# The last step of a spiking recurrence: its final gather as a piece of its own, the reset operand by thirds, Newton's step in two operations

## The chip, the cores and the metric

The kernel runs on one core of a Trainium2 chip. The metric is the device time of one execution in microseconds (us). The time before is the median of three executions. The profile is of one more execution, with a time of its own.

## The reference, cut to what matters

1024 users (B) each have a sequence of 50 item numbers (T). An item number selects a row of a table of 100001 items by 128 features (D); row 0 counts as zeros.

```
e      = emb[seq]                                  # [B, T, D]
uF     = cumsum(e, axis=1) / min(t, length)        # running mean
y      = (uF - mean_B(uF)) * rsqrt(var_B(uF) + 1e-5) * gamma + beta
for t in range(50):                                # v starts at zero
    v = v + (y[:, t] - v) / 2
    spike = (v >= 1);  v = v - spike;  count += spike
scores = (count / 50) @ emb.T                      # [1024, 100001], float32
```

The mean and the variance are taken over the 1024 users, for each feature and each step. The recurrence is short in bytes; the scores are 409.6 MB of output.

## The kernel before, in words

**Layout.** In the recurrence the 128 partitions are the features and the 1024 columns are the users, in eight blocks of 128. PSUM holds the running sums in `pre[0]` and `pre[1]` (512 columns each), the spike counts in `sums[0]` and `sums[1]`, and two buffers of 1024 columns, `v0` and `v1`, in which the steps' `v` alternate: even steps in `v0`, odd ones in `v1`.

**One step t.** GpSimd (POOL) issues eight indirect DMAs for step t+1, one for each block of users (`gather`, L198), into `e`. TensorE (PE) transposes each block of `e` and adds it into `pre` (L307). VectorE (DVE) turns each half of `pre` into the running mean `uF` (L316) and takes its statistics (`bn_stats`, L317), and `bn_aggr` (L327) joins the two halves to mean and variance, `mv`. ScalarE (ACT) takes the square root of the variance (L331) and subtracts the mean from `uF` (L332). DVE forms the scale `a` by four operations of one column after a reciprocal and a Newton step (L340 to L346): `r = 1/r`, `q = r*r`, `q = (var+eps)*q`, `q = 1.5-0.5*q`, `a = q*r*...`. ACT writes the scaled input into `v` (L350, `x`). DVE adds half of the old `v` after its reset (L353, `step`), which needs `negv = spike - v` of the step before (L359).

**The spikes of the step before** are taken by DVE (`s`, L337), and PE adds them into `sums` by a product with the identity (`counted`, L275). In the steps up to 48 this stands between `bn_aggr` and the reciprocal.

**The last step** (t = 49) differs. Its `s` (L301) and its whole `negv` (L302) come first on DVE, ahead of `uF`. `counted` stands on PE behind all eight transposes, and ACT copies `sums` to `count` (L325). Sixteen transposes into a spare tile, `warm` (L376), fill PE's time until the first product. Then the 1024 columns are handled in three groups of 128, 512 and 384: `x` of all three on ACT, then on DVE `step` and `spiked` of the first group (giving `countA`), `step` of the two others, and `spiked` of the two others (`countB`, `countC`, L286). The operands `v` of the groups lie in `pre[0]`, `pre[1]` and `vC`, which takes the buffer `v1`; `warm` takes `v0`.

**The scores.** For every piece of 1024 items the table's rows are transposed (L128) and split into a high and a low part (L150, L151); PE multiplies them with the counts (L158) for eight blocks of users; DVE (L467) and ACT (L469) evict by turns, and SyncE's queue stores (L167). Users of block 0 come first, from `countA`, by four evictions of 512 columns (L401, L403) that use `sums` and a tile `po1` in `v0`. The blocks after it use `countB` and `countC`. Ahead of the recurrence's end two pieces of items have been split already.

**Order.** Each engine runs its instructions in the order in which the program gives them; nothing is rescheduled. A tile's reuse waits for the last instruction that used it.

Of the kernel before, what the change touches and what calls it, by code (L numbers as in the profile page):

```python
# [12 lines left out]
F32 = mybir.dt.float32  # L13
# [5 lines left out]
ALU = mybir.AluOpType  # L19

P = 128
BN_EPS = 1e-5
V_TH = 1.0
HALF = 1024
KQ = HALF // P
BANK = 512
# [10 lines left out]
def rec_kernel(  # L37
# [9 lines left out]
    nc = tc.nc  # L47
    B, T = seq.shape
    N, D = table.shape
    NB = B // P  # L50
# [119 lines left out]
    with ExitStack() as ph:  # L170
        once = ph.enter_context(tc.tile_pool(name="once", bufs=1))
        lp = ph.enter_context(tc.tile_pool(name="lif", bufs=2))
        sp = ph.enter_context(tc.tile_pool(name="stats", bufs=3))
# [3 lines left out]
        vp = ph.enter_context(tc.tile_pool(name="v", bufs=1, space=bass.MemoryType.PSUM))  # L177
# [16 lines left out]

        def gather(t):
            es[t] = gp.tile([P, B], F32, tag="e", name=f"e_{t}")
            for n in range(NB):
                nc.gpsimd.indirect_dma_start(  # L198
                    out=es[t][:, n * P : (n + 1) * P],
                    out_offset=None,  # L200
                    in_=table,
                    in_offset=bass.IndirectOffsetOnAxis(ap=idx[:, n, t : t + 1].bitcast(U32), axis=0),
                )
# [34 lines left out]
        rlen = once.tile([P, B], F32, tag="rlen", name="rlen")  # L238
# [10 lines left out]
        negv = once.tile([P, B], F32, tag="negv", name="negv")  # L249
# [3 lines left out]
        pre = [accp.tile([P, BANK], F32, tag=f"pre{h}", name=f"pre{h}") for h in range(B // BANK)]  # L253
# [19 lines left out]
        def counted(t, s):  # L273
            for h in range(B // BANK):
                nc.tensor.matmul(  # L275
                    sums[h],
                    lhsT=ident_h,
                    rhs=s[:, h * BANK : (h + 1) * BANK],
                    start=t == 0,
                    stop=t == T - 2,  # L280
                    skip_group_check=True,
                )


        def spiked(out, cs, v):
            nc.vector.scalar_tensor_tensor(out, v, V_TH, count[:, cs], ALU.is_ge, ALU.add)  # L286

        whole = slice(0, B)
        halves = [slice(h * BANK, (h + 1) * BANK) for h in range(B // BANK)]
        v = None  # L290
# [3 lines left out]
        for t in range(T):  # L294
            last = t == T - 1
            if t + 1 < T:
                gather(t + 1)
            e = es.pop(t)
            if last:
                s = lp.tile([P, B], BF16, tag="s", name=f"s_{t - 1}")  # L300
                nc.vector.tensor_single_scalar(s, v, V_TH, ALU.is_ge)  # L301
                nc.vector.tensor_tensor(negv, s, v, ALU.subtract)  # L302
            uF = up.tile([P, B], F32, tag="uF", name=f"uF_{t}")
            bs = sp.tile([P, B // BANK, 6], F32, tag="bs", name=f"bs_{t}")
            for h, cs in enumerate(halves):
                for k in range(0, BANK, P):
                    nc.tensor.matmul(  # L307
                        pre[h][:, k : k + P],
                        lhsT=e[:, h * BANK + k : h * BANK + k + P],
                        rhs=ident,  # L310
                        start=False,
                        stop=last,
                        is_transpose=True,
                        skip_group_check=True,
                    )
                nc.vector.scalar_tensor_tensor(uF[:, cs], rlen[:, cs], 1.0 / (t + 1), pre[h], ALU.max, ALU.mult)  # L316
                nc.vector.bn_stats(bs[:, h, :], uF[:, cs])  # L317
            if not last:
                correct(t + 1, l)
            else:  # L320

                counted(t - 1, s)
                count = once.tile([P, B], F32, tag="zT", name="count")
                for h, cs in enumerate(halves):
                    nc.scalar.copy(count[:, cs], sums[h])  # L325
            mv = sp.tile([P, 2], F32, tag="mv", name=f"mv_{t}")
            nc.vector.bn_aggr(mv, bs.rearrange("p h s -> p (h s)"))  # L327


            r = sp.tile([P, 1], F32, tag="r", name=f"r_{t}")  # L330
            nc.scalar.activation(r, mv[:, 1:2], AF.Sqrt, bias=eps)  # L331
            nc.scalar.activation(uF, uF, AF.Identity, bias=mv[:, 0:1], scale=-1.0)  # L332


            if t and not last:
                s = lp.tile([P, B], BF16, tag="s", name=f"s_{t - 1}")
                nc.vector.tensor_single_scalar(s, v, V_TH, ALU.is_ge)  # L337
                counted(t - 1, s)

            nc.vector.reciprocal(r, r)  # L340
            q = sp.tile([P, 1], F32, tag="q", name=f"q_{t}")
            nc.vector.tensor_mul(q, r, r)
            nc.vector.scalar_tensor_tensor(q, mv[:, 1:2], BN_EPS, q, ALU.add, ALU.mult)
            nc.vector.tensor_scalar(q, q, -0.5, 1.5, ALU.mult, ALU.add)
            a = sp.tile([P, 1], F32, tag="a", name=f"a_{t}")
            nc.vector.tensor_scalar(a, q, r, hgb[:, 0:1], ALU.mult, ALU.mult)  # L346


            def x(vt, cs):
                nc.scalar.activation(vt, uF[:, cs], AF.Identity, bias=hgb[:, 1:2], scale=a)  # L350

            def step(vt, cs):
                nc.vector.scalar_tensor_tensor(vt, negv[:, cs], -0.5, vt, ALU.mult, ALU.add)  # L353

            if not last:
                vt = vp.tile([P, B], F32, tag=f"v{t % 2}", name=f"v_{t}")
                x(vt, whole)
                if t:
                    nc.vector.tensor_tensor(negv, s, v, ALU.subtract)  # L359
# [11 lines left out]

        warm = vp.tile([P, HALF], F32, tag="v0", name="warm")
        for k in range(2 * KQ):
            nc.tensor.transpose(warm[:, k % KQ * P : (k % KQ + 1) * P], ident, ident)  # L376
        vC = vp.tile([P, B - BANK - P], F32, tag="v1", name="vC")
        groups = [
            (slice(0, P), pre[0][:, :P], countA),
            (slice(P, P + BANK), pre[1], countB),  # L380
            (slice(P + BANK, B), vC, countC),
        ]
        for cs, vt, _ in groups:
            x(vt, cs)
        cs, vt, first = groups[0]
        step(vt, cs)
        spiked(first, cs, vt)
        for cs, vt, _ in groups[1:]:
            step(vt, cs)
        for cs, vt, c in groups[1:]:  # L390
# [118 lines left out]
```

## Time and profile before

| | |
|---|---|
| median of three runs | 1647.41 us (1646.87 to 1650.15) |
| profiled execution, its own time | 1574.98 us |
| its span, first to last instruction | 1573.2 us |
| mean granted TensorE clock | 0.966 |
| busy shares of the span | PE 73%, DVE 60%, ACT 40%, POOL 24% |
| gathers on POOL | 400 of 945 ns each |
| stores | 409.60 MB written |

The span has two stages. In the first, up to about 505 us, POOL issues one gather after the other and the other engines follow it, at about 10 us a step. In the second the scores are written: between 600 and 700 us the DMA engines are fully busy and move 420 GB/s. The last step of the recurrence and the first products are the joint between the two.

### The profile page before, as it was taken

To read this page: it belongs to the slowest core of one execution; us is meant where nothing else is said; L and a number is where in the kernel's file an instruction comes from. 1 tells how busy PE (TensorE), PEld (TensorE's weight loads), DVE (VectorE), ACT (ScalarE), POOL (GpSimd) and SP (SyncE) were. 2 spreads that over 40 slices of the span, in tenths; PEclk is the share of its full clock that TensorE was granted. 3 is DMA by queue.
4 is the path that set the end of the run, shared out by engine and by line. 5 is a ranking of instruction groups with operands and counts; after the bars stand their busy time and mean duration, and the time that the engine had idled before them with its cause. 6 is when DMAs were issued, how large, how long until landed. Compare 5 with 4: busy or idle time off the path is not lost.

```text
span 1573.2 us, 12601 instructions
## 1 busy us (share of the span) xinstructions
PE 1147.9 (73%) x4538; PEld 817.6 (52%) x4548; DVE 942.1 (60%) x1161; ACT 630.6 (40%) x700; POOL 378.5 (24%) x406
## 2 busy tenths in 40 slices
PE   4555555555555998889878878887888778777885
PEld 2222222222233776668667666666666667665763
DVE  4777777777777665667555545545555555554553
ACT  2322222222233554555444444444444444443442
POOL 6777777777776000000000000000000000000000
PEclk9999999999999999999999999999999999999998
DMA  9622222222221999999999999999999999999898
GB/s 338 247 53 53 53 53 52 53 53 53 53 79 45 385 416 403 423 417 402 426 429 428 430 427 424 421 415 428 418 428 423 414 428 410 426 424 426 362 423 371
DMA packets 54859, 488.14 MB, mean 310 GB/s; under 512 B 12139, under 2 KB 12940, under 8 KB 32524
## 3 DMA queue, kind: packets, MB, share of 16 engines
q1 hardware_dynamic: 33424, 429.81, 65.1%
q0 software_dynamic: 12800, 26.24, 6.3%
q10 hardware_dynamic: 8572, 31.28, 5.0%
q8 instruction: 36, 0.59, 0.1%
q14 instruction: 27, 0.22, 0.0%
HBM read 77.69 MB, written 409.60 MB: 310 GB/s over the span
## 4 chain that ended last, share of the span: by engine, by line
DMA 50%; POOL 19%; PE 11%; issue 10%; ACT 5%; DVE 4%; another core or an unknown queue 0%; DVEq 0%; ACTq 0%; SPq 0%; POOLq 0%
DMA scores<-o 46%; POOL e L198 19%; PE po L158 10%; ACT o L469 4%; DMA e<-in_L_rec_emb_table,idx 3%; DVE o L467 2%; DMA rows<-in_L_rec_emb_table 2%; PE pt L128 1%; PE pre L307 0%; ACT pairs L150 0%; DVE s L337 0%; DVE bs L317 0%; DVE uF L316 0%; DVE pairs L151 0%; DMA idx<-in_r_seq 0%
## 5 line engine op out<-in xcount | busy, mean ns | idle before, releaser
L467 DVE TENSOR_SCALAR o<-po 128x1024 f32<-128x1024 f32 x391 | 464.1, 1220 | 354.3 <-DMA scores<-o 314.5
L469 ACT ACTIVATE o<-po 128x1024 f32<-128x1024 f32 (+1 forms) x391 | 388.1, 1019 | 548.9 <-DMA scores<-o 336.2
L198 POOL DMA_INDIRECT e<-in_L_rec_emb_table,idx x400 | 377.8, 945 | 124.5 <-issue 116.4
L158 PE MATMUL po<-pairs,countB 128*128 128x512 f32 x1136 | 304.6, 415 | 69.0 <-ACT o L469 52.1
L158 PEld LDWEIGHTS po<-pairs,countB 128*128 128x128 f32 x1136 | 218.5, 197 | 132.0 <-ACT o L469 66.8
L307 PE MATMUL pre<-ident,e 128*128 128x128 f32 x400 | 156.2, 452 | 152.4 <-DMA e<-in_L_rec_emb_table,idx 149.0
L158 PE MATMUL po<-pairs,countC 128*128 128x512 f32 x852 | 230.4, 416 | 49.3 <-ACT o L469 49.3
L158 PEld LDWEIGHTS po<-pairs,countC 128*128 128x128 f32 x852 | 163.6, 198 | 94.2 <-ACT o L469 60.5
L307 PEld LDWEIGHTS pre<-ident,e 128*128 128x128 f32 x400 | 79.2, 200 | 246.1 <-DMA e<-in_L_rec_emb_table,idx 223.6
L151 DVE TENSOR_TENSOR pairs<-pt,pairs 128x1024 fp32r<-128x1024 f32 x71 | 86.3, 1222 | 91.3 <-ACT pairs L150 91.2
L331 ACT ACTIVATE r<-mv,eps 128x1 f32<-128x1 f32 x50 | 14.7, 295 | 305.5 <-DVE mv L327 305.5
L316 DVE SCALAR_TENSOR_TENSOR uF<-rlen,pre 128x512 f32<-128x512 f32 x100 | 68.4, 684 | 108.3 <-PE pre L307 108.2
L128 PE MATMUL pt<-ident,rows 128*128 128x128 f32 x782 | 111.7, 290 | 9.7 <-ACT o L469 5.1
L128 PEld LDWEIGHTS pt<-ident,rows 128*128 128x128 f32 x782 | 100.3, 152 | 29.9 <-issue 8.8
L158 PE MATMUL po<-hi,countB 128*128 128x512 f32 x216 | 89.5, 414 | 15.8 <-ACT o L469 12.6
L264 PE MATMUL pre<-zT,l 128*128 128x512 f32 x100 | 78.1, 783 | 18.9 <-DVE uF L316 18.8
L275 PE MATMUL sums<-s,ident_h 128*128 128x512 bf16 x88 | 45.4, 607 | 60.6 <-DVE s L337 60.6
L158 PE MATMUL po<-lo,countB 128*128 128x512 f32 x216 | 86.5, 402 | 0.0
L158 PE MATMUL po<-pairs,countA 128*128 128x512 f32 x284 | 71.7, 395 | 9.3 <-ACT o L469 9.2
L150 ACT CAST pairs<-pt 128x1024 fp32r<-128x1024 f32 x71 | 71.8, 1012 | 15.0 <-PE pt L128 14.8
L158 PE MATMUL po<-hi,countC 128*128 128x512 f32 (+1 forms) x162 | 67.8, 418 | 11.7 <-ACT o L469 11.7
L350 ACT ACTIVATE v<-uF,hgb,a 128x1024 f32<-128x1024 f32 x49 | 59.2, 1208 | 37.6 <-DVE a L346 37.5
(76 smaller groups left out, 841.9 us busy)
## 6 DMA issues: line engine op xcount, KB each, us to landing
scores<-o SPq DMA_DIRECT2D x88, 3072.0 KB, 20.3
scores<-o SPq DMA_DIRECT2D x32, 1536.0 KB, 8.9
scores<-o SPq DMA_DIRECT2D x16, 2048.0 KB, 12.6
scores<-o SPq DMA_DIRECT2D x30, 1024.0 KB, 8.6
rows<-in_L_rec_emb_table ACTq DMA_DIRECT2D x19, 1536.0 KB, 29.3
rows<-in_L_rec_emb_table SPq DMA_DIRECT2D x6, 3072.0 KB, 25.3
scores<-o SPq DMA_DIRECT2D x8, 1872.5 KB, 11.3
e<-in_L_rec_emb_table,idx POOLq DMA_INDIRECT x400, 2.5
```

Source lines behind the costliest of these rows:

```text
L128: nc.tensor.transpose(pt[:, k0 : k0 + kw], r[:kw, k0 : k0 + D], ident[:kw, :kw])
L150: nc.scalar.copy(vh, vp)
L151: nc.vector.tensor_tensor(vl, vp, vh.bitcast(F32), ALU.subtract)
L158: nc.tensor.matmul(po[:, :kw], lhsT=counts[n], rhs=part[:, k0 : k0 + kw], start=j == 0, stop=j == 1,)
L198: nc.gpsimd.indirect_dma_start(out=es[t][:, n * P : (n + 1) * P], out_offset=None, in_=table, in_offset=bass.IndirectOffsetOnAxis(ap=idx[: ...
L264: nc.tensor.matmul(pre[h], lhsT=l, rhs=zT[:, h * BANK : (h + 1) * BANK], start=t == 0, stop=False, skip_group_check=True,)
L275: nc.tensor.matmul(sums[h], lhsT=ident_h, rhs=s[:, h * BANK : (h + 1) * BANK], start=t == 0, stop=t == T - 2, skip_group_check=True,)
L307: nc.tensor.matmul(pre[h][:, k : k + P], lhsT=e[:, h * BANK + k : h * BANK + k + P], rhs=ident, start=False, stop=last, is_transpose=True, ...
L316: nc.vector.scalar_tensor_tensor(uF[:, cs], rlen[:, cs], 1.0 / (t + 1), pre[h], ALU.max, ALU.mult)
L350: nc.scalar.activation(vt, uF[:, cs], AF.Identity, bias=hgb[:, 1:2], scale=a)
L467: nc.vector.tensor_scalar_mul(o[:, h0 : h0 + hw], po[:, :hw], 1.0 / T)
L469: nc.scalar.mul(o[:, h0 : h0 + hw], po[:, :hw], 1.0 / T)
```

## The change

Five things are edited.

- The last gather's order of blocks becomes 0, 1, 2, 3, 5, 6, 7, 4. Its `uF` and `bn_stats` are taken in three pieces: 512 columns (blocks 0 to 3), 384 columns (blocks 5 to 7) and 128 columns (block 4, the one that comes last).
- `counted` of the step before, on PE, moves ahead of the transpose of block 4.
- `negv` of the last step is no longer taken whole ahead of `uF`: the first 128 columns follow `bn_aggr`, the next 512 follow `a`, the last 384 follow `countA`.
- In every step, `ve = var + eps` is formed on DVE right after `bn_aggr`, and the Newton step's two products become one operation, `q = (r*ve)*r`.
- `warm` takes the buffer `v1` in place of `v0`, since the old `v` in `v0` is now read later.

```diff
 def gather(t):
-            for n in range(NB):
+            order = list(range(NB))
+            if t == T - 1:
+                order.append(order.pop(NB // 2))
+            for n in order:
...
+        thirds = [slice(0, P), slice(P, P + BANK), slice(P + BANK, B)]
+
+        def negated(cs):
+            nc.vector.tensor_tensor(negv[:, cs], s[:, cs], v[:, cs], ALU.subtract)
...
                 nc.vector.tensor_single_scalar(s, v, V_TH, ALU.is_ge)
-                nc.vector.tensor_tensor(negv, s, v, ALU.subtract)
...
-            for h, cs in enumerate(halves):
-                for k in range(0, BANK, P):
+            pieces = halves if not last else halves[:1] + [slice(B - 3 * P, B), slice(BANK, BANK + P)]
+            bs = sp.tile([P, len(pieces), 6], F32, tag="bs", name=f"bs_{t}")
+            for j, cs in enumerate(pieces):
+                h = cs.start // BANK
+                if last and j == len(pieces) - 1:
+                    counted(t - 1, s)
+                for c0 in range(cs.start, cs.stop, P):
+                    k = c0 - h * BANK
                     nc.tensor.matmul(
...
-                nc.vector.bn_stats(bs[:, h, :], uF[:, cs])
+                nc.vector.bn_stats(bs[:, j, :], uF[:, cs])
             if not last:
                 correct(t + 1, l)
             else:
-                counted(t - 1, s)
...
             nc.scalar.activation(r, mv[:, 1:2], AF.Sqrt, bias=eps)
+            ve = sp.tile([P, 1], F32, tag="ve", name=f"ve_{t}")
+            nc.vector.tensor_scalar_add(ve, mv[:, 1:2], BN_EPS)
...
+            if last:
+                negated(thirds[0])
             nc.vector.reciprocal(r, r)
-            nc.vector.tensor_mul(q, r, r)
-            nc.vector.scalar_tensor_tensor(q, mv[:, 1:2], BN_EPS, q, ALU.add, ALU.mult)
+            nc.vector.scalar_tensor_tensor(q, r, ve, r, ALU.mult, ALU.mult)
...
-        warm = vp.tile([P, HALF], F32, tag="v0", name="warm")
+        warm = vp.tile([P, HALF], F32, tag="v1", name="warm")
...
+        negated(thirds[1])
         for cs, vt, _ in groups:
             x(vt, cs)
         cs, vt, first = groups[0]
         step(vt, cs)
         spiked(first, cs, vt)
+        negated(thirds[2])
         for cs, vt, _ in groups[1:]:
             step(vt, cs)
```

More of the change, by code (lines that the diff above doesn't have):

```diff
@@ L301, in rec_kernel @@
                 nc.vector.tensor_single_scalar(s, v, V_TH, ALU.is_ge)
-                nc.vector.tensor_tensor(negv, s, v, ALU.subtract)
             uF = up.tile([P, B], F32, tag="uF", name=f"uF_{t}")
-            bs = sp.tile([P, B // BANK, 6], F32, tag="bs", name=f"bs_{t}")
-            for h, cs in enumerate(halves):
-                for k in range(0, BANK, P):
+            pieces = halves if not last else halves[:1] + [slice(B - 3 * P, B), slice(BANK, BANK + P)]
[6 more added lines that the diff above has]
+                    k = c0 - h * BANK
                     nc.tensor.matmul(
                         pre[h][:, k : k + P],
-                        lhsT=e[:, h * BANK + k : h * BANK + k + P],
+                        lhsT=e[:, c0 : c0 + P],
                         rhs=ident,
@@ L315, in rec_kernel @@
                     )
-                nc.vector.scalar_tensor_tensor(uF[:, cs], rlen[:, cs], 1.0 / (t + 1), pre[h], ALU.max, ALU.mult)
-                nc.vector.bn_stats(bs[:, h, :], uF[:, cs])
+                nc.vector.scalar_tensor_tensor(
+                    uF[:, cs],
+                    rlen[:, cs],
+                    1.0 / (t + 1),
+                    pre[h][:, cs.start - h * BANK : cs.stop - h * BANK],
+                    ALU.max,
+                    ALU.mult,
+                )
+                nc.vector.bn_stats(bs[:, j, :], uF[:, cs])
             if not last:
@@ L358, in rec_kernel @@
                 if t:
-                    nc.vector.tensor_tensor(negv, s, v, ALU.subtract)
+                    negated(whole)
                 step(vt, whole)
@@ L377, in rec_kernel @@
         vC = vp.tile([P, B - BANK - P], F32, tag="v1", name="vC")
[L378 to L382, printed above, removed]
+        groups = list(zip(thirds, (pre[0][:, :P], pre[1], vC), (countA, countB, countC)))
+        negated(thirds[1])
         for cs, vt, _ in groups:
```

## The prediction, made before the changed kernel ran

> **What bounds the kernel now.** I read the waits first, to learn who paces the two stages, then the chain of waits through the joint between them, then the timeline there.
>
> The steps before the last are paced by POOL. Two rows of the waits (engine, line, waited for: us in total, times, longest):
>
> ```profile
> POOL e L198 <- issue: 116.4, 382, 0.3
> DVE uF L316 <- PE pre L307: 108.2, 47, 3.5
> ```
>
> POOL waits almost only for its own next issue: 945 ns and 0.30 us of gap, eight times, make 10 us a step. DVE waits 108.2/47 = 2.3 us in each step for the last transposes. So a DVE or ACT operation in steps 0 to 48 has 2.3 us of cover.
>
> The last step differs. Rows of the chain of waits there (start us, us, what):
>
> ```profile
> 500.86 1.24 DVE v L353
> 502.13 1.24 DVE s L301
> 503.38 1.22 DVE negv L302
> 504.60 0.61 DVE uF L316
> 505.24 0.69 DVE bs L317
> 505.93 0.60 DVE uF L316
> 506.55 0.71 DVE bs L317
> 507.28 0.22 DVE mv L327
> ```
>
> The reader is to see that DVE never waits here. The last gather's block is transposed in time: the timeline (start, us, engine, line) has it ending at 505.79, while DVE is busy to 505.93.
>
> ```profile
> 505.31 0.48 PE L307 MATMUL pre<-ident,e 128*128 128x128 f32 x1 [0.88 <-DMA e<-in_L_rec_emb_table,idx]
> 505.58 1.06 PE L275 MATMUL sums<-s,ident_h 128*128 128x512 bf16 x2
> 507.52 0.29 ACT L331 ACTIVATE r<-mv,eps 128x1 f32<-128x1 f32 x1 [0.20 <-DVE mv L327]
> 507.72 1.13 ACT L332 ACTIVATE uF<-uF,mv 128x1024 f32<-128x1024 f32 x1
> 507.85 0.16 DVE L340 RECIPROCAL r<-r 128x1 f32<-128x1 f32 x1 [0.36 <-ACT r L331]
> 508.63 0.27 DVE L346 TENSOR_SCALAR a<-q,r,hgb 128x1 f32<-128x1 f32 x1
> 509.49 0.30 DVE L353 SCALAR_TENSOR_TENSOR pre<-negv,pre 128x128 f32<-128x128 f32 x1 [0.59 <-ACT pre L350]
> 509.82 0.29 DVE L286 SCALAR_TENSOR_TENSOR countA<-pre,count 128x128 fp32r<-128x128 f32 x1
> 511.26 0.69 DVE L286 SCALAR_TENSOR_TENSOR countB<-pre,count 128x512 fp32r<-128x512 f32 x1
> ```
>
> After that the scores are bound by the stores. Two windows (stretch, length, busy times, clock, DMA share, GB/s) show how soon:
>
> ```profile
> 512.00:526.00 14.00, 13.51 (x65) 10.93 (x64) 9.39 (x9) 7.69 (x9) 0.00 (x0) 1.00 0.86 344
> 526.00:546.00 20.00, 18.58 (x88) 13.98 (x87) 12.06 (x10) 10.41 (x12) 0.00 (x0) 1.00 1.01 419
> ```
>
> To 526 us PE sets the pace (13.51 of 14 us busy); from there DMA is full. What is won at the joint moves all stores earlier by as much; nothing that the change touches lies behind it, where each engine's order of operations stays as it was. The whole joint, `s` to the first product, is 8 us, 0.5% of the span, so no edit in it can bring much.
>
> **The change, part by part**, in the profiled execution's own times.
>
> *Steps 0 to 48.* `ve` is one 128x1 operation like L342 to L344 (0.15 to 0.16 us). It waits for `mv`, so it starts some 0.24 us after `bn_aggr` does, and `s`, which followed 0.13 us after, starts about 0.23 later. One product less behind the reciprocal gives back one pitch, 508.24 - 508.05 = 0.19. Net +0.04 us on `a` in each step, under the 2.3 us cover: 0. Uncovered it would be 48 x 0.04 = 2 us. In step 48 there is no such cover, since the last step's `s` follows at once: +0.04.
>
> *`negv` leaves DVE's head.* `s` runs 502.17 to 503.39. `uF` of blocks 0 to 3 starts at about 503.40, not 504.52, and its `bn_stats` at 504.12. `uF` of blocks 5 to 7 (384 columns, as the 0.56 of `vC` in L353) runs 504.81 to 505.37; block 7, now the seventh gather, was transposed in that place at 503.96 to 504.44. Its `bn_stats` ends near 505.95. So DVE alone would let block 4 in at 505.95.
>
> *Block 4 on PE.* Its gather is still issued eighth and lands at 505.25. Two things now stand ahead of it: `counted`, and a wait for DVE's read of blocks 5 to 7, since they share `pre[1]` (the built program has that wait). The read ends at 505.37. `counted` starts after block 7, at about 504.55, and holds PE as long as before, from 505.58 to `warm`'s start at 506.43, 0.85 us: to about 505.4 to 505.6. I take a transpose from 505.55 to 506.03. Queued behind it are `warm` and the first product. Bounds: it can start no earlier than the landing allowed before (505.31, when DVE's 505.95 decides) and, with `counted` at its full 1.06 us and a late issue, at 505.85. So `uF` of block 4 starts at 506.08, between 505.95 and 506.40.
>
> *Statistics.* Two operations of 128 columns (0.30 us each by L353's first group, pitch 0.33) in place of two of 512 (pitch 0.70): `bn_aggr` starts at 506.08 + 0.66 = 506.74, not 507.28. That is -0.54 (-0.67 to -0.2).
>
> *Root and Newton.* `r` comes 0.57 us after `bn_aggr` starts (507.85 - 507.28). But `ve` (0.24 to about 0.40) and 128 columns of `negv` (0.30) now stand ahead of the reciprocal: it starts at 0.70, 0.13 late. Newton's missing operation returns 0.19. `a` starts at 508.03: -0.60. ACT's subtraction (L332) keeps its distance and ends at 508.30, just ahead of `x` at 508.40, so no more than 0.1 us could have been had here. The copies to `count` end near 506.3, ahead of `r` at 506.98; before they ended at 507.32, 0.2 us ahead of it.
>
> *First group.* 512 columns of `negv` (0.70, as L353's 512) now stand behind `a`, from 508.28 to 508.97. `x` of the first group, 0.38 us as ACT's 128 columns in `l`, is done at 508.8; `step` waits 0.1 us more for DVE: 508.97, not 509.49. `countA` starts at 509.30: -0.52. `warm`, 3.62 us from 506.05, ends at 509.67; the product could start at 509.72. This cover is thin: each 0.1 us that block 4 is later than I take it shifts the product by 0.1.
>
> *Groups two and three.* 384 columns of `negv` (0.56) stand behind `countA`. `x` of the third waits for `warm`'s end and is done by 510.4. `step` of the second starts at 510.12, not 510.19; `countB` is ready 0.07 earlier, at 511.88. PE ends the first block's products at 511.64 and waits 0.3 us for it. This is covered: the next piece on PE waited before too, for the eviction L401 (PE restarted at 513.73), and that eviction follows the first block's products: 512.47, not 512.99, when DVE is free of `countC` (512.35). So the shift of -0.52 is passed on. If it were not, -0.07 would be left.
>
> **The sum**: -0.52 us. Below it, block 4 at its earliest (0.13), a reciprocal that isn't late (0.13) and a `step` that doesn't wait (0.1) make -0.9. Above it, only the -0.07 of `countB` is passed on, and block 4 is at its latest (0.32): +0.25. The span of 1573.2 becomes 1572.7 and the profiled time 1574.98 becomes 1574.5. The median before, 1647.41, lies 72.4 us (4.6%) above the profiled time; the trace can't show where, and I carry the microseconds over unscaled: 1646.9. About 0.2%, or 3.3 us, is what a measurement of this kernel can tell from no change, and the sum is a sixth of that.
>
> [...] L353's groups of 512, 384 and 128 columns take 0.70, 0.56 and 0.30 us: about 0.17 us fixed and 1.03 ns a column. [...]
>
> The reciprocal's successors stand 0.19 to 0.20 us apart though one column takes little work. [...] The rows show `ve` beside ACT's root, so I count the 0.19.
>
> **The rivals.**
>
> *The gain is lost at the joint* (chance 0.25): `countB`'s 0.07 sets the pace of all later blocks, or block 4 comes late. For it: `negv` costs 1.56 us in thirds against 1.22, two of them in the chain. Against: PE's stall for L401. Time 1647.3, at worst 1647.9 in the late case, which I give 0.05 of its own.
>
> *Slower over the bound* (0.07): `ve` ahead of `s` in every step. If DVE's cover of 2.3 us is not there in the timed executions, the steps pay 0.23 each without Newton's return: 49 x 0.23 = 11.3 us, 1658.7; with it 49 x 0.04 = 2 us, 1649.4. It decides only from the point where DVE's wait for PE in a step falls to nothing; the row of 108.2 us says that it is far off.
>
> *Faster over the bound* (0.08): the chain through `a` paces the steps, and each gains Newton's 0.19: 9.5 us, 1637.9. Against it stands POOL's row.
>
> *It doesn't do what it says*: block 4 is alone in its piece, but its transpose waits for the other piece's evacuation. That is in my sum; if DVE and not the gather still ends last, the time is that of the first rival.
>
> **How the numbers follow.** My forecast has 0.55, its own range 1646.5 to 1647.5; with the first rival and the late case 0.85 lie within 0.5 us of no change. The three runs lie up to 2.74 us from their median (1650.15), so of these 0.85 I put 0.06 beyond the bound as faster and 0.04 as slower. Faster 0.08 + 0.06 = 0.14, slower 0.07 + 0.04 = 0.11, within 0.75. The range is 1646.5 - 2.7 to 1647.9 + 2.7: 1643.8 to 1650.6.
>
> **What would show it.** `bn_aggr` of the last step 4.6 us after `s` (before 5.15); block 4's transpose right behind `counted`; the reciprocal 0.70 after `bn_aggr`; `countA` about 7.1 us after `s` starts (before 7.69); PE's stall before the second piece kept; DMA full about 0.5 us sooner. It is wrong if DVE's wait in the steps is gone, if the first product waits for `warm`, or if the store stage itself is longer or shorter by microseconds.

## The result, and the profile after

| kernel | median, us | lowest to highest | ratio to before, 95% interval |
|---|---|---|---|
| before | 1648.26 | 1646.87 to 1650.15 | |
| changed | 1645.51 | 1645.20 to 1646.64 | 0.9984 [0.9966, 1.0001] |

The changed kernel came out 2.75 us shorter by the medians, 2.6 by the ratio, where 0.52 was forecast. Two repetitions of the same pair, told below, gave 0.9985 [0.9974, 0.9997] and 0.9990 [0.9974, 1.0006]. So the gain lies near 2 to 2.5 us; one of the three intervals excludes no change.

One thing is needed to compare traces: chips differ. On those that time the kernel before at 1648 to 1651 us the steps take about 575 us, and the last gathers have landed early when the last step begins. In the profile shown ahead of the prediction (1575 us, its chip is not on record) the steps take 502 us and the last gather lands late. The changed kernel's profile is of the first kind, so it is compared below with a second profile of before of that kind (own time 1651.8 us, span 1650.0).

The header and the granted clock, of the changed kernel (own time 1645.49 us) in 40 slices:

```profile
span 1643.7 us, 12618 instructions
PE 1108.6 (67%) x4548; PEld 825.2 (50%) x4548; DVE 945.6 (58%) x1165; ACT 630.2 (38%) x700; POOL 378.3 (23%) x406
PEclk9975555555555599999999999999999999998998
```

and the same row of the first profile of before:

```profile
PEclk9999999999999999999999999999999999999998
```

That row, and the mean clock of 0.966 in the table ahead of the prediction, mislead. The first clock record in that trace starts at 509.92 us, 7.80 us after the last `s` starts; ahead of it the row shows 9 with no record behind it, as in the first two slices of the changed kernel's row. What TensorE did there shows the half clock. The first line below is that profile's stretch from 20 to 500 us, the second the same stretch of `thirds_only`, told below, whose record has 0.50 (the three last numbers: granted clock, DMA share, GB/s); the third is `warm` of the first profile.

```profile
20.00:500.00 480.00, 250.73 (x587) 116.29 (x596) 346.80 (x635) 141.31 (x197) 362.90 (x385) 1.00 0.29 85
20.00:500.00 480.00, 253.11 (x596) 116.01 (x596) 346.57 (x634) 141.51 (x197) 362.74 (x385) 0.50 0.29 85
506.43 3.62 PE L376 MATMUL warm<-ident 128*128 128x128 f32 x16
```

PE is busy for 0.43 us an instruction in the one (250.73/587) and 0.42 in the other. The 16 transposes start 0.21 us apart, as the changed kernel's do (below) while its record says 0.50; in `before_warm26` they go from 0.21 to 0.11 when the record changes to 1.00. So the steps ran at half clock in the first profile too, and the two kinds of profile differ in when the last gathers land, and not by a full clock in the steps (the changed kernel's and the second profile of before have 0.60 and 0.56 in the same stretch).

The waits of the changed kernel that answer to the two rows in the prediction (us in total, times, longest):

```profile
DVE uF L332 <- remote: 154.8, 30, 9.8
POOL e L201 <- issue: 112.8, 370, 0.3
POOL e L201 <- remote: 65.3, 18, 5.4
```

"remote" stands where the profile finds no releaser on this core. DVE's 108.2 us of waits for PE have become 154.8 us of waits for something that comes up to 9.8 us late. That is no effect of the change: the second profile of before has the same rows.

```profile
DVE uF L316 <- remote: 142.4, 27, 9.3
POOL e L198 <- remote: 63.9, 15, 5.6
```

Because the step stage moves by microseconds between executions (the last `s` starts at 576.95 us in this profile of before and at 573.34 in the changed kernel's), the joint is read from the start of that `s`. The joint of the changed kernel, from the timeline (start, us, engine, line, operation, idle time ahead and its releaser):

```profile
573.34 1.22 DVE L310 TENSOR_SCALAR s<-v 128x1024 bf16<-128x1024 f32 x1
...
574.62 1.01 PE L278 MATMUL sums<-s,ident_h 128*128 128x512 bf16 x2 [2.14 <-DVE s L310]
...
576.39 0.48 PE L323 MATMUL pre<-ident,e 128*128 128x128 f32 x1 [0.76 <-DVE uF L332]
...
576.66 3.62 PE L400 MATMUL warm<-ident 128*128 128x128 f32 x16
...
577.56 0.24 DVE L348 BATCH_NORM_AGGREGATE mv<-bs 128x2 f32<-128x18 f32 x1
577.83 0.15 DVE L354 TENSOR_SCALAR ve<-mv 128x1 f32<-128x1 f32 x1
577.90 0.28 DVE L295 TENSOR_TENSOR negv<-s,v 128x128 f32<-128x128 bf16 x1
578.03 1.13 ACT L355 ACTIVATE uF<-uF,mv 128x1024 f32<-128x1024 f32 x1
578.16 0.16 DVE L365 RECIPROCAL r<-r 128x1 f32<-128x1 f32 x1
578.80 0.27 DVE L370 TENSOR_SCALAR a<-q,r,hgb 128x1 f32<-128x1 f32 x1
579.20 1.16 ACT L374 ACTIVATE pre<-uF,hgb,a 128x128 f32<-128x128 f32 x2
580.02 0.29 DVE L289 SCALAR_TENSOR_TENSOR countA<-pre,count 128x128 fp32r<-128x128 f32 x1
580.46 0.76 PE L158 MATMUL sums<-hi,countA 128*128 128x512 f32 x1 [0.18 <-ACT pre L374]
581.02 0.48 PE L158 MATMUL sums<-lo,countA 128*128 128x512 f32 x1
581.34 0.39 PE L158 MATMUL sums<-hi,countA 128*128 128x512 f32 x1
```

`bn_aggr` stands 4.22 us after `s` and `countA` 6.68, where the prediction's times, 506.74 and 509.30, make 4.61 and 7.17 (the row has `s` at 502.13; the prediction once says 502.17). Block 4's transpose waits for DVE's read, and `warm` follows it and ends at 580.28, just ahead of the first product. From the third product on the spacing is 0.23 us. The second profile of before, same view:

```profile
576.95 1.22 DVE L301 TENSOR_SCALAR s<-v 128x1024 bf16<-128x1024 f32 x1
...
578.23 1.01 PE L275 MATMUL sums<-s,ident_h 128*128 128x512 bf16 x2 [2.06 <-DVE s L301]
...
579.49 3.67 PE L376 MATMUL warm<-ident 128*128 128x128 f32 x16 [0.25 <-DVE negv L302]
...
585.08 0.77 PE L158 MATMUL sums<-hi,countA 128*128 128x512 f32 x1 [1.93 <-ACT pre L350]
585.65 0.63 PE L158 MATMUL sums<-lo,countA 128*128 128x512 f32 x1
586.08 0.63 PE L158 MATMUL sums<-hi,countA 128*128 128x512 f32 x1
```

Here the last gathers have landed early and all eight transposes are over (the last starts at 575.75), so `warm` runs right behind `counted`. Then PE idles 1.93 us, and the products come 0.43 us apart, almost twice as far as in the other kernel. Two windows each from the first products on, first of before and then of the changed kernel; the last three numbers are the granted clock, the DMA share and GB/s:

```profile
584.00:588.00 4.00, 2.92 (x7) 2.37 (x8) 2.81 (x6) 2.78 (x5) 0.00 (x0) 0.50 0.05 19
588.00:592.00 4.00, 4.00 (x12) 2.90 (x12) 1.92 (x2) 0.70 (x2) 0.00 (x0) 0.60 0.65 243
```

```profile
581.00:585.00 4.00, 3.52 (x15) 2.57 (x14) 3.33 (x6) 1.68 (x3) 0.00 (x0) 0.98 0.50 185
585.00:589.00 4.00, 4.00 (x24) 3.37 (x23) 1.61 (x2) 2.65 (x3) 0.00 (x0) 1.00 0.85 339
```

The joint in numbers, in us after the start of the last `s`. "Block 1" is PE's first product of the second piece of items after its stall, the earliest point that carries all that the joint won; "end" is the end of the span.

| profile | `bn_aggr` | `countA` | first product | `warm` | clock full | block 1 | end |
|---|---|---|---|---|---|---|---|
| before, first | 5.15 | 7.70 | 8.13 | 4.31 to 7.93 | 7.8 | 11.61 | 1071.1 |
| before, second | 5.15 | 7.69 | 8.13 | 2.54 to 6.21 | 14.2 | 13.39 | 1073.1 |
| changed | 4.22 | 6.68 | 7.12 | 3.32 to 6.94 | 7.9 | 10.97 | 1070.4 |

Against the second profile of before, PE is 1.01 us sooner at the first product and 2.42 us sooner at block 1, and the span's end follows by 2.7. About 1 us is the shorter joint that was forecast (larger than forecast); some 1.4 us more is the clock during the first products, which the forecast did not have. In the first profile of before `warm` ends 0.21 us ahead of the first product and the clock is up in time, so that profile could not show the loss.

### The profile page after: what moved, and what is told of

Same layout as the page of the kernel before. It is cut to its first block, busy times and chain, and to the rows that moved or that the text cites. A ratio compares the mean times of both kernels' runs of the same rounds, so it can differ in the third digit from the quotient of the medians.

```text
span 1643.7 us, 12618 instructions
## 1 busy us (share of the span) xinstructions
PE 1108.6 (67%) x4548; PEld 825.2 (50%) x4548; DVE 945.6 (58%) x1165; ACT 630.2 (38%) x700; POOL 378.3 (23%) x406
## 4 chain that ended last, share of the span: by engine, by line
DMA 47%; DVE 23%; another core or an unknown queue 11%; PE 9%; ACT 6%; issue 3%; DVEq 0%; POOL 0%; ACTq 0%; SPq 0%; POOLq 0%
DMA scores<-o 46%; PE po L158 9%; DVE bs L340 4%; ACT o L491 4%; DVE uF L332 4%; DVE v L377 4%; DVE s L360 3%; DVE negv L295 3%; DVE o L489 2%; DVE a L370 1%; DMA e<-in_L_rec_emb_table,idx 1%; DVE mv L348 1%; DVE q L367 1%; ACT v L374 0%
## 5 line engine op out<-in xcount | busy, mean ns | idle before, releaser
L267 PE MATMUL pre<-zT,l 128*128 128x512 f32 x100 | 74.4, 746 | 251.3 <-DVE uF L332 203.5
L267 PEld LDWEIGHTS pre<-zT,l 128*128 128x128 f32 x100 | 27.7, 278 | 291.3 <-issue 175.0
L332 DVE SCALAR_TENSOR_TENSOR uF<-rlen,pre 128x512 f32<-128x512 f32 (+1 forms) x101 | 68.1, 674 | 167.5 <-remote 154.8
L323 PE MATMUL pre<-ident,e 128*128 128x128 f32 x400 | 102.1, 423 | 15.9 <-DMA e<-in_L_rec_emb_table,idx 13.8
L323 PEld LDWEIGHTS pre<-ident,e 128*128 128x128 f32 x400 | 85.7, 224 | 47.7 <-DMA e<-in_L_rec_emb_table,idx 23.9
L278 PE MATMUL sums<-s,ident_h 128*128 128x512 bf16 x98 | 49.6, 609 | 75.4 <-DVE s L360 44.3
```

The lines of the kernel that those rows point to most:

```text
L267: nc.tensor.matmul(pre[h], lhsT=l, rhs=zT[:, h * BANK : (h + 1) * BANK], start=t == 0, stop=False, skip_group_check=True,)
L323: nc.tensor.matmul(pre[h][:, k : k + P], lhsT=e[:, c0 : c0 + P], rhs=ident, start=False, stop=last, is_transpose=True, skip_group_check=True,)
```

## The experiments

Kernels that are compared in one paragraph's ratios ran on one chip with the kernel before. A ratio and the two medians beside it can give gains up to 1 us apart; the ratio has the interval, so it is the ratio that is compared.

**Did it come from the joint or from the Newton step?** Four kernels on one chip (before 1647.69 us). `after_again` is the changed kernel once more.

> The changed kernel once more, in more rounds. In its first profile the joint (start of the last step's spike operation to start of countA) took 6.68 us against 7.69 before, and PE restarted on the second piece after 10.97 us against 11.60, so 0.63 us should reach the stores. Theory A (only the joint counts): 0.6 us faster, ratio 0.9996, between 0.999 and 1.000. Theory B (the 2.7 us between the first medians are real, and 2 us of them come from the steps): ratio 0.9984. Theory C (scatter): ratio 1.000 within 0.0005 either way.

Measured: 1645.72 us, 0.9985 [0.9974, 0.9997]. `bn_aggr` 4.22, `countA` 6.68, block 1 at 10.60. The gain repeats.

`joint_only` keeps all but the Newton step:

```
-            ve = sp.tile([P, 1], F32, tag="ve", name=f"ve_{t}")
-            nc.vector.tensor_scalar_add(ve, mv[:, 1:2], BN_EPS)
...
-            nc.vector.scalar_tensor_tensor(q, r, ve, r, ALU.mult, ALU.mult)
+            nc.vector.tensor_mul(q, r, r)
+            nc.vector.scalar_tensor_tensor(q, mv[:, 1:2], BN_EPS, q, ALU.add, ALU.mult)
```

> The change without the new Newton step: the four operations of one column as before in all steps, everything else of the change kept. Theory A: the joint to countA is 7.0 us or less (before 7.69), since behind the reciprocal one product returns (0.14 to 0.19 us) but ve (0.07 to 0.25) no longer delays; 0.5 to 0.9 us faster than before. Theory B: the gain of the steps is gone, no more than 0.6 us faster, while the Newton step alone is 2 us faster.

Measured: 1646.17 us, 0.9986 [0.9972, 1.0001]; `countA` 6.79, first product 7.22, block 1 at 11.53, clock full at 9.0. The joint's edits alone give the whole gain within the interval. The Newton step is worth 0.11 us on `countA`; the rest of the 0.93 us by which block 1 is later than in `after_again` is the clock, which came up after the first products here.

`newton_only` is the reverse, the kernel before with only these lines changed:

```
+            ve = sp.tile([P, 1], F32, tag="ve", name=f"ve_{t}")
+            nc.vector.tensor_scalar_add(ve, mv[:, 1:2], BN_EPS)
...
-            nc.vector.tensor_mul(q, r, r)
-            nc.vector.scalar_tensor_tensor(q, mv[:, 1:2], BN_EPS, q, ALU.add, ALU.mult)
+            nc.vector.scalar_tensor_tensor(q, r, ve, r, ALU.mult, ALU.mult)
```

> The kernel before with nothing but ve = var + eps and Newton's step in two operations, in all 50 steps. In the traces a step whose gathers have landed, and which DVE's chain alone paces, takes 7.50 us before and 7.58 after. Theory A: if 30 of the 50 steps are of that kind and this is passed on, up to 2.4 us slower; if POOL or late landings pace them, no change within 1 us. Theory B: 2 us faster.

Measured: 1647.97 us, 1.0006 [0.9997, 1.0015]. No gain, so the theory that the Newton chain paces the steps falls. Its groups show why the return was smaller than I took it (count, then busy us in total, mean ns):

```profile
L344 DVE SCALAR_TENSOR_TENSOR q<-r,ve 128x1 f32<-128x1 f32 x50 | 11.0, 221 | 1.8
L333 DVE TENSOR_SCALAR ve<-mv 128x1 f32<-128x1 f32 x50 | 7.7, 153 | 1.7
```

The merged operation takes 221 ns where the two products of before took 159 and 165. The steps in which DVE waits for nothing but 0.2 us for ACT last 7.584 us on average, against 7.486 in the second profile of before: +0.10 where +0.04 was forecast. The interval, from -0.5 to +2.5 us, can't tell whether that is covered, but two traces from one other chip can. There, two such steps and the long one behind them take 34.0 us together (median of 13 such groups) both in the second profile of before, with the old Newton step, and in `after_no_warm`, with the new one. The late releases set that pace, and the +0.10 is covered.

**Are the late releases in the steps a matter of buffers?** `gather3` is the changed kernel with a third buffer for the gathers:

```
-        gp = ph.enter_context(tc.tile_pool(name="gather", bufs=2))
+        gp = ph.enter_context(tc.tile_pool(name="gather", bufs=3))
```

> The changed kernel with three gather buffers in place of two. In the profile of the changed kernel POOL stood 65 us waiting for a buffer, and some steps took 17 us where others took 7.6. If the late releases are a delay that can be overlapped, POOL runs on without a pause, the steps take about 505 us in place of 575, and the time falls by 50 to 70 us. The rival: each late release costs its 10 us whatever lies ahead, and the time stays within 5 us.

Measured: 1647.84 us, 1.0013 [1.0002, 1.0024]. A miss: no faster than before, and slower than the changed kernel beside it. POOL waits as before:

```profile
POOL e L201 <- remote: 66.6, 18, 6.5
```

So a gather buffer that comes free late is not what holds the steps.

**Is the second half of the gain TensorE's clock?** Four kernels on another chip (before 1651.38 us). First the second profile of before itself, which is the one read above:

> The kernel before, unchanged, for a profile of the state in which the timed runs are. Theory W (warm): as in the run with Newton's step alone, the gathers of the last step have landed early, the sixteen warm transposes run from 2.5 to 5.5 us after the last spike operation starts, PE then idles 2.5 us, and the first eight products run 0.43 us apart in place of 0.23; PE restarts on the second piece at 13.0 to 13.2 us, where the changed kernel has 10.6 to 11.0. Theory A (joint only): PE restarts at 11.6 us as in the first profile.

Its own time was 1651.8 us. The clock theory says: on such chips `warm` ends too early in the kernel before, so the first products run at half clock, and the changed kernel's wait for DVE's read is what keeps `warm` next to the first product. Then the kernel before should gain nearly as much from a longer `warm` alone. `before_warm26`:

```
-        for k in range(2 * KQ):
+        for k in range(2 * KQ + 10):
             nc.tensor.transpose(warm[:, k % KQ * P : (k % KQ + 1) * P], ident, ident)
```

> The kernel before with 26 warm transposes in place of 16, so that they end about 2 us later and leave PE less than 1 us of idle time before the first product; nothing else is changed. Theory W: the first products run 0.23 us apart, PE restarts on the second piece 1.2 to 1.6 us sooner, and the time falls by as much, ratio 0.9990 to 0.9993. Theory A: no change, or slower where the transposes hold the first product.

Measured: 1650.12 us, 0.9986 [0.9975, 0.9996], -2.3 us by the ratio and -1.3 by the medians, with nothing else changed. Its timeline:

```profile
577.28 1.22 DVE L301 TENSOR_SCALAR s<-v 128x1024 bf16<-128x1024 f32 x1
...
579.82 4.34 PE L376 MATMUL warm<-ident 128*128 128x128 f32 x26 [0.25 <-DVE negv L302]
...
585.41 0.47 PE L158 MATMUL sums<-hi,countA 128*128 128x512 f32 x1 [1.26 <-ACT pre L350]
585.72 0.40 PE L158 MATMUL sums<-lo,countA 128*128 128x512 f32 x1
```

The first product stands at 8.13 us after `s`, exactly where it stood, but the spacing is 0.23 us at once (clock full at 5.2), and block 1 comes at 11.62 instead of 13.39: 1.77 us from the clock alone. Behind `warm`'s 1.26 us of idle time the clock was still up. Behind a longer one it was not: in `newton_only`, where the 16 transposes stand as in the second profile of before and 2.50 us of idle time follow, the clock was up at 4.7, back at half at 8.1, and block 1 came at 13.09.

The other side of the same test is the changed kernel without the 16 transposes of `warm`, `after_no_warm`:

```
-        warm = vp.tile([P, HALF], F32, tag="v1", name="warm")
-        for k in range(2 * KQ):
-            nc.tensor.transpose(warm[:, k % KQ * P : (k % KQ + 1) * P], ident, ident)
```

> The changed kernel without the sixteen warm transposes, so that PE idles 3.5 us between block 4 and the first product; the order on DVE and ACT is that of the changed kernel. Theory W: countA at 6.7 us as in the changed kernel, but the first products 0.43 us apart, and 1.5 to 2 us of the gain are lost: ratio to the kernel before 0.9996 to 1.0000. Theory A: the gain is that of the changed kernel, 0.9985.

Measured: 1650.93 us, 0.9996 [0.9986, 1.0006].

```profile
580.05 0.48 PE L323 MATMUL pre<-ident,e 128*128 128x128 f32 x1 [0.77 <-DVE uF L332]
...
584.11 0.77 PE L158 MATMUL sums<-hi,countA 128*128 128x512 f32 x1 [3.59 <-ACT pre L374]
584.67 0.63 PE L158 MATMUL sums<-lo,countA 128*128 128x512 f32 x1
```

The first product stands at 7.12 as in the changed kernel, but PE had idled 3.59 us: the spacing is 0.43 us until 10.6, and block 1 comes at 12.24. Against the 10.60 of `after_again`, 1.64 us are gone in the trace; the changed kernel itself was not timed on this chip. Against the second profile of before, 1.15 us are left, which the interval (-2.3 to +1.0 us) can't tell from no change.

**The parts of the joint one by one.** `pieces_only` is the kernel before with the last gather's order, the three pieces and the early `counted`, but with the whole `negv` ahead of `uF`, `warm` in `v0` and the old Newton step:

```
+            if t == T - 1:
+                order.append(order.pop(NB // 2))
...
-                nc.vector.tensor_tensor(negv, s, v, ALU.subtract)
+                negated(slice(0, B))
...
+            pieces = halves if not last else halves[:1] + [slice(B - 3 * P, B), slice(BANK, BANK + P)]
...
+                if last and j == len(pieces) - 1:
+                    counted(t - 1, s)
```

> The last gather in the new order with three pieces and the earlier product of the counts, but negv whole and first as before, the old Newton step, and warm in its old buffer. countA then comes 0.3 us later than before (about 8.0 us after the spike operation). Theory W: since block 4's transpose now waits for DVE's read of the other three blocks of its bank, warm starts at about 4.6 us and ends at 7.9, right before the first product; the products run 0.23 us apart, PE restarts at about 12 us, and the kernel is 1 us faster than before although countA is later. Theory A: 0.3 us slower.

Measured: 1650.85 us, 1.0001 [0.9992, 1.0010], by the medians -0.5 us. In its trace `bn_aggr` is at 5.48 and `countA` at 8.04, 0.35 later than before, because DVE has a piece more to do and nothing is taken from its head; `warm` runs from 4.58 to 8.20 and block 1 comes at 11.98, 1.41 sooner than in the second profile of before. That is what the clock theory wants of the trace, but the time does not show it: -1.41 us would be 0.9991, just below the interval. I count it as inconclusive; it speaks against the theory's size, not against the two runs before it.

`thirds_only` has the reverse: `negv` by thirds and `warm` in `v1`, with the old order, halves, `counted` and Newton step:

```
-                nc.vector.tensor_tensor(negv, s, v, ALU.subtract)
...
+            if last:
+                negated(thirds[0])
...
+        negated(thirds[1])
...
+        negated(thirds[2])
```

> negv by thirds and warm in its new buffer, but the last gather in its old order and halves, the product of the counts behind all eight transposes, and the old Newton step. DVE's head is then 1.2 us shorter: countA 6.6 to 6.8 us after the spike operation starts, as in the changed kernel. But nothing holds the warm transposes back: they start about 2.2 us after the spike operation and end near 5.5. Theory W: PE idles over 1 us before the first product, many products run 0.43 us apart, and PE restarts on the second piece at 12.0 to 12.6 us, where the changed kernel has 10.6 to 11.0 and the one before 13.4; ratio 0.9993 (0.9990 to 0.9998). Theory A: the products are not affected, PE restarts at 11 us.

Measured: 1574.83 us against 1575.03 for before on this chip, 0.9999 [0.9990, 1.0008]. The chip was one of the quicker kind, where the gathers pace the steps and the last one lands late (its transpose, at 505.11, waits 0.70 us for it), so the expected `countA` was missed:

```profile
501.93 1.23 DVE L308 TENSOR_SCALAR s<-v 128x1024 bf16<-128x1024 f32 x1
...
505.62 0.69 DVE L327 SCALAR_TENSOR_TENSOR uF<-rlen,pre 128x512 f32<-128x512 f32 x1 [1.14 <-PE pre L318]
...
509.61 0.29 DVE L287 SCALAR_TENSOR_TENSOR countA<-pre,count 128x128 fp32r<-128x128 f32 x1
```

DVE, freed of `negv`, only waits 1.14 us longer for the last transposes; `countA` stands at 7.68 as before. There the thirds are worth nothing without the order. On a chip of the other kind `pieces_only` shows that the order is worth nothing on `countA` without the thirds. So neither was worth anything on `countA` alone where it ran; what the thirds alone do where the gathers land early, no run shows.

**On the quicker chip.** `filler` was meant to raise the clock in the steps: the changed kernel with two extra transposes of the identity behind each block from the fourth on, in steps 2 to 48, whose results are not used:

```
+            if 1 < t < T - 1:
+                fill = vt = vp.tile([P, B], F32, tag=f"v{t % 2}", name=f"v_{t}")
...
+                    if fill is not None and c0 >= 3 * P:
+                        for i in range(2):
+                            nc.tensor.transpose(fill[:, i * P : (i + 1) * P], ident, ident)
```

> The changed kernel with ten transposes of the identity more in each step from 2 to 48, two behind each block from the fourth on, into the tile that the step's v will overwrite; their results are not used. In the first profile of the kernel before, PE had full clock in the steps and they took 10.0 us; in all profiles since, half clock, and they took 11.5 us on average, with late releases. If the half clock is a cause of the late releases, the steps go back to about 10 us and the time falls by 50 to 75 us. The rival: the releases are late for another reason; then the time stays, or rises by what the fillers hold up, at most 20 us.

Measured: 1574.05 us against 1575.03, 0.9994 [0.9984, 1.0004], -1.0 us. Its steps took 10.0 us as those of before do on this chip, so it says nothing on the late releases. Its premise was the misread row as well: the first profile of before had no full clock in the steps, and the fillers hardly raised it (0.54 between 20 and 500 us, against 0.50 in `thirds_only`). But its last step is the changed kernel's where the gathers land in time, the situation that I predicted for:

```profile
504.13 1.06 PE L278 MATMUL sums<-s,ident_h 128*128 128x512 bf16 x2
...
505.24 0.18 PEld L326 LDWEIGHTS pre<-ident,e 128*128 128x128 f32 x1 [0.95 <-DVE uF L338]
505.27 0.45 PE L326 MATMUL pre<-ident,e 128*128 128x128 f32 x1
...
506.40 0.24 DVE L354 BATCH_NORM_AGGREGATE mv<-bs 128x2 f32<-128x18 f32 x1
...
508.86 0.29 DVE L289 SCALAR_TENSOR_TENSOR countA<-pre,count 128x128 fp32r<-128x128 f32 x1
```

With `s` at 502.15, `bn_aggr` is at 4.25, `countA` at 6.72 and block 1 at 10.66, against 5.15, 7.70 and 11.61 in the first profile of before: -0.95 us at block 1, which agrees with the -1.0 us of the time; seven of its eight times lie below all 27 of before. The changed kernel without fillers was not run on this chip.

**A version of my own.** `best` is the changed kernel with the old Newton step in steps 0 to 48 and eight transposes more, ahead of `counted`, to bring the clock up sooner:

```
+                    early = vp.tile([P, HALF], F32, tag="v1", name="early")
+                    for i in range(KQ):
+                        nc.tensor.transpose(early[:, i * P : (i + 1) * P], ident, ident)
                     counted(t - 1, s)
```

> The changed kernel with the old Newton step in steps 0 to 48 (the new one in the last step alone), and with eight more transposes of the identity on PE ahead of the product of the counts, where PE idles 2 us in the last step. Theory W: PE is at full clock before the first product, which starts at 7.1 us after the spike operation; PE restarts on the second piece at 10.6 us in every run, where the changed kernel had 11.0 or 10.6. Steps that DVE's chain paces take 7.48 us, not 7.58; if 28 of them count, 2.8 us more. Ratio to the kernel before 0.9970 to 0.9985; the changed kernel's was 0.9985.

Measured, on the same quicker chip: 1575.47 us, 1.0003 [0.9994, 1.0012]. A miss:

```profile
503.91 1.92 PE L321 MATMUL early<-ident 128*128 128x128 f32 x8
505.62 1.06 PE L278 MATMUL sums<-s,ident_h 128*128 128x512 bf16 x2
506.47 0.42 PE L325 MATMUL pre<-ident,e 128*128 128x128 f32 x1
506.93 0.29 DVE L334 SCALAR_TENSOR_TENSOR uF<-rlen,pre 128x128 f32<-128x128 f32 x1 [1.56 <-PE pre L325]
```

The eight transposes stand on PE ahead of block 4, which moves from 505.27 in `filler` to 506.47; DVE waits 1.56 us for it and `countA` falls back to 8.26. Here, work that only warms the clock belonged behind block 4, for which DVE waits.

**Once more, on a third chip of the first kind**, the changed kernel unaltered:

> The changed kernel once more. Where the gathers land in time and the steps take 10.0 us (kernel before 1575 us): the joint is that of the run with fillers, countA 6.7 us after the spike operation and PE's restart at 10.7 to 11.0 us, against 7.69 and 11.6 before; warm ends right before the first product in both kernels, so the gain is the joint's alone, 0.6 to 1.0 us, ratio 0.9994 to 0.9996. Where the gathers land late (kernel before about 1648 us): ratio 0.9985 as before, of which the products at full clock make 1.8 us.

Measured: 1645.96 us against 1648.06, 0.9990 [0.9974, 1.0006]; `countA` 6.68, clock full at 5.8, block 1 at 10.59. DVE's and ACT's rows repeat those of `after_again` to 0.01 us up to the first product.

## Why the prediction was right or wrong

**The number.** 1645.51 us lies in the stated range, 1643.8 to 1650.6, but that range holds 2.7 us on each side for the scatter of runs; the forecast's own 1646.5 to 1647.5 was missed. That the time lies inside is in part luck: of the 2.6 us gained, about 1.0 is the mechanism that was forecast, and the rest is one that was not.

**What held.** The direction and the mechanism of the joint. Block 4's transpose does wait for DVE's read of the other piece (0.76 us idle in the changed kernel's row; in `filler` its weight load waits 0.95 us for that read). The step operation still follows `negv` closely, `warm` still ends ahead of the first product (6.94 against 7.12: the thin cover held), and PE's stall ahead of the second piece is kept (0.48 us behind L423), so what the first block won is passed on. The wait for `countB` that was foreseen behind the first block is there where the clock is up (0.2 us in `filler`), and it is covered. The rival that loses the gain at the joint falls with it. `newton_only` (+0.0006) shows neither the slower rival's 11.3 us nor the faster rival's 9.5 us.

**The term of block 4 was too late by 0.36 us.** Forecast 4.61 for `bn_aggr`, measured 4.25 in `filler`, where the gathers land as in the profile that I worked from. DVE's read ended 3.00 us after `s`, not 3.24, since each of DVE's operations ahead of it follows the one before sooner than the pitch that I took; the transpose came 0.12 behind the read, not 0.18, and `uF` 0.48 behind it, not 0.53. So DVE's read decided, and not `counted`.

**The reciprocal was taken 0.1 too late, Newton's return 0.05 too large.** The reciprocal stands 0.60 behind `bn_aggr`, not 0.70: `ve` and the first piece of `negv` start 0.07 us apart. From the reciprocal to `a` it is 0.64 us, before 0.78: a return of 0.14, not 0.19, because one merged operation costs 221 ns. And it buys little here: ACT's subtraction runs to 579.16 and `x` starts at 579.20, while `a` is done at 579.07. I had put that limit 0.1 us away; it is now the bound.

**The sum for the joint** was -0.52 with bounds of -0.9 and +0.25; `filler` gave -0.95 at block 1 and -1.0 [-2.5, +0.6] in time. The two terms above make up most of the difference, and the lower bound was about right. The added operations cost the joint little, because they stand where DVE waited before: `ve` and the first piece of `negv` lie beside ACT's root (the reciprocal stands 0.60 us behind `bn_aggr`, 0.57 in the first profile of before), and the second piece fills the 0.59 us for which DVE waited for `x` (the step operation stands 0.89 us behind `a`, 0.86 in that profile).

**The term that was missing is TensorE's clock.** I took the products' 0.23 us spacing and `warm`'s place from a profile in which the last gather lands late, so that `warm` meets the first product and brings the clock up just ahead of it (7.80 against 8.13), and carried the microseconds over to timed executions that are 72 us longer without knowing what fills these. It is the step stage, and at its end the last gathers are in early, `warm` is over 1.93 us before the first product, and the clock is at half when the products start. There the wait that I charged as a pure cost, block 4 behind DVE's read, is an advantage: it holds `warm` back until it meets the first product. That is worth 13.39 - 11.62 = 1.77 us by `before_warm26` and 12.24 - 10.60 = 1.64 us by `after_no_warm`. With the joint's 1.0 the sum is -2.6 to -2.8 us, where the three ratios give -2.6, -2.5 and -1.6 (the medians -2.8, -2.0 and -2.1). The second half was argued from traces first and then shown by two runs with one edit each; `pieces_only` is the one run whose time doesn't follow its trace.

**The cover of 2.3 us in each step** was that profile's too. In the changed kernel's profile 28 of the 49 steps last 7.58 us and DVE does not wait for the gathers in them. The +0.10 us that they got is still covered, by the late releases and not by the wait that I named.

**What stays open**: why releases come up to 10 us late in the steps on most of these chips. A third gather buffer changed nothing, and a half clock alone does not make it: `thirds_only` and the first profile of before had the clock at half in the steps too and still took 10.0 us a step. No run here has the steps at full clock.

## What to carry to other kernels

Ask of every gain at a joint whether the profile that you work from is in the same condition as the timed runs: a difference of 4.6% between the two was a sign that terms of the sum, here the place of `warm` and with it the matmul spacing, could not be carried over. Check a clock row against the spacing of equal instructions before building on it: here a full clock in the row was a lack of records. Ask of warm-up work whether the clock is up when what it is for begins. Here the products ran 0.23 us apart where 16 transposes ended 0.18 us ahead of them (changed kernel, from the third product on) and where 26 ended 1.26 us ahead (`before_warm26`), and 0.43 us apart where 16 ended 1.93 us ahead (second profile of before) or 2.50 us (`newton_only`). So look at the spacing of the first matmuls behind it, and try its length (one number here was worth most of what the whole change was). When an operation is taken off one engine's head, look for the limit of another engine at almost the same time: here `negv` by thirds alone left `countA` at 7.68 us and the new order alone at 8.04, against 7.70 and 7.69 before; together, in `joint_only`, they had 6.79.

## What the runs showed of the hardware that was not expected

The same 16 transposes of `warm`, 3.6 us, raised the clock when they started 3.3 us after `s` and met the first product, and did not when they started at 2.5 and 1.9 us of idle time followed: there it stayed at half until 14.2. In `newton_only` the same early place did raise it, at 4.7, but it fell back at 8.1 and rose again at 11.5: these points lie 3.41 us apart. Twenty-six transposes did it with 1.26 us idle behind them. For one and the same order of instructions the clock was full at 7.9, 6.3 and 5.8 us in three profiles. The first and the last of these lie about 2 us apart, and 3.6 us of transposes were enough in some places and not in others; what sets the point no run here shows. Products of 512 columns came 0.43 us apart where the record has 0.50 (second profile of before, 584 to 588 us) and 0.23 us where it has 1.00 (changed kernel, 585 to 589 us).

A step of the recurrence took 10.0 us on one chip, while on others one or two steps of about 7.5 us, which DVE paces, were mostly followed by one of 17 to 19 us in which DVE and POOL wait for a release that the profile can't name. That is 72 us of 1648, thirty times what the change is worth.
